# Two-layer graph network over 128 graphs: graph layers beside the next group's first feed-forward, attention two groups ahead beside the second

## The chip, the cores and the metric

The kernel runs on one core of one Trainium2 chip. The metric is the device time of one execution in microseconds (us), lower is better. The engines are called as the profile calls them: PE is TensorE (matmuls), PEld its weight loads, DVE is VectorE, ACT is ScalarE, POOL is GpSimd, SP is SyncE, which here only issues DMAs.

## The reference, cut

The input holds 128 graphs of 128 nodes with 256 features, and one 0/1 adjacency matrix for each graph. Layer 0 is an attention whose values are chosen by the adjacency entry (four relations, of which 0 and 1 occur), followed by a feed-forward with Gelu. Layer 1 is two graph-attention steps in a row, followed by a feed-forward with Relu. Each half of a layer ends in a layer norm. All is float32.

```python
# layer 0; h = 8 heads of dh = 32
scores = jnp.einsum('bhid,bhjd->bhij', q, k) / np.sqrt(dh)
attn = jax.nn.softmax(scores, axis=-1)
for r in range(Wv.shape[0]):
    v_r = (src @ Wv[r] + bv[r]).reshape(Bb, Nn, h, dh).transpose(0, 2, 1, 3)
    mask = (adj_matrix == r)[:, None]
    out = out + jnp.einsum('bhij,bhjd->bhid', attn * mask, v_r)
attn_out = out.transpose(0, 2, 1, 3).reshape(Bb, Nn, Dm) @ Wo + bo
x = _ln(src + attn_out, g1, beta1)
ff = jax.nn.gelu(x @ W1 + b1, approximate=False) @ W2 + b2
return _ln(x + ff, g2, beta2)

# layer 1
def _gat(h, adj, W, a, out_features):
    Wh = jnp.matmul(h, W)
    e = Wh @ a[:out_features] + jnp.swapaxes(Wh @ a[out_features:], 1, 2)
    e = jax.nn.leaky_relu(e, negative_slope=ALPHA)
    att = jax.nn.softmax(jnp.where(adj > 0, e, NEG), axis=1)
    return jnp.matmul(att, Wh)
h = _gat(_gat(x, adj, W1, a1, Fout), adj, W2, a2, W2.shape[1])
h = _layernorm(x + h, g_ln1, b_ln1)
ff = jnp.matmul(jax.nn.relu(jnp.matmul(h, w_ff1) + b_ff1), w_ff2) + b_ff2
return _layernorm(h + ff, g_ln2, b_ln2)
```

## The kernel before

The 128 graphs are taken in 32 groups of four (G = 4), so a group is 512 tokens. A group runs through these stages; "unit" is the kernel's word for a piece of a feed-forward.

- Projections (in `layer0`): two matmul pairs for q, two for k (`pq`, L382, emptied by ACT at L386) and four for the values of relation 0 and of the difference of relations 1 and 0 (`pv`, L392, emptied by DVE at L396).
- Attention (`scores`, `attended`), twice, each for two graphs: scores for four head groups into four tiles `ps` (L319), exponential on ACT (L326), product with the adjacency on DVE (L327), sums with a matrix of ones (`pden`, L342), weighted values (`pav`, L352), reciprocal (L359) and product (L362) on DVE. Then the output projection `pwo` in two halves (L412), each added to the residual on DVE (`added`, L270) into `t0`.
- Layer norm (`normed`): statistics on DVE (L237, L238), the power −0.5 on POOL (L241), subtraction and product on DVE (L243). `scaled` makes the residual of the next stage on POOL (L250, L251), `transposed` turns the normed tile for the next matmuls: eight transposes on PE into two tiles `pt` (L260), each emptied by ACT (L263).
- Feed-forward (`ffn`): eight units `ph` of two matmuls (L280), each followed by Gelu or Relu on ACT (L284), then two halves `po` of four units (L291), each half added by DVE.
- Graph layer (`layer1`): `pw` and `pb` (L452, L459), a chain of edge scores (`edges`: ACT L423, DVE L426, ACT exponential L427, DVE L430 to L436, POOL L437), `py` and `pb` (L467, L471), a second chain of edge scores, and `pg` (L482), added into `t2`.

PE's order is written out by hand (`manual_schedule` for PE alone); a scheduler orders the other engines' queues at build time, and each queue runs in order on the chip. `beside` interleaves: the side generator yields how many units of the feed-forward come next. In the main loop (L541), turn g pairs the first feed-forward of group g with the attention of group g + 1 (`turn`, with the transposes of group g − 1 after the four q and k projections), then the second feed-forward of group g − 1 with the graph layer of group g. So at g = 0 the graph layer has nothing beside it, nor has the first group's attention.

PSUM tiles are of [128, 512] float32. Pool `ps_s` has four (tag `s`: `ps`, `pt`, `pw`, `py`, `pg`), `ps_mm` two (tag `mm`: `pq`, `pv`, `ph`, `po`, `pwo`), and `ps_av` one for tag `av` and one for `den`. A tile's place is taken again when the engine that empties it is done.

At the start the weights are loaded on SP's queue, the bias vectors as rows and columns on ACT's queue; at the end of these loads come the weights of the graph layer (L191, L192), from which DVE and PE make combined weights (L193 to L219) ahead of all other PE work. The residual `res`, `t` and the transposed `yT` tiles have three buffers each, `hT` one.

At the end a check of sums and variances is reduced to one flag (L567 to L590); a general version of the kernel runs only if the flag is set.

Of the kernel before, what the change touches and what calls it, by code (L numbers as in the profile page):

```python
# [10 lines left out]
F32 = mybir.dt.float32  # L11
# [14 lines left out]
G = 4  # L26
# [4 lines left out]
class Weights:  # L31


    def __init__(self, tc, const, a):
        self.tc, self.nc, self.const, self.a = tc, tc.nc, const, a

# [10 lines left out]
    def col(self, name):  # L47
        v = self.a[name]
        t = self.tile([P, v.shape[0] // P], "c_" + name)
        with self.nc.allow_non_contiguous_dma(reason="a bias vector as columns"):  # L50
            self.nc.scalar.dma_start(t, v.rearrange("(c p) -> p c", p=P))
        return t

    def row(self, name, first=None, t=None):
        v = self.a[name]
        n = 1
        for s in v.shape:
            n *= s
        n = first or n
        if t is None:  # L60
            t = self.tile([P, n], "r_" + name)
        self.nc.scalar.dma_start(
            t, bass.AP(tensor=v.tensor, offset=v.offset, ap=[[0, P], [1, n]])
        )
        return t
# [38 lines left out]
def fast_pass(ctx, tc, a, out):  # L104
# [27 lines left out]
    def load(g):  # L132
        xt = io.tile([P, NCH, T], F32, tag="xT", name=f"xT_{g}")
        nc.sync.dma_start(
            xt, xT[:, g * T : (g + 1) * T].rearrange("(c p) t -> p c t", p=P)
        )
        ad = w3p.tile([P, G, P], I32, tag="adj", name=f"adj_{g}")
        nc.sync.dma_start(ad, adjT[:, g * G : (g + 1) * G, :])
        xr = io.tile([P, G, D], F32, tag="x", name=f"x_{g}")
        nc.sync.dma_start(  # L140
            xr, x[g * T : (g + 1) * T, :].rearrange("(b p) d -> p b d", p=P)
        )
        return xt, ad, xr


    k.constants()
    wq, wk = k.w("L0_gnn_Wq"), k.w("L0_gnn_Wk")
    first = dict(zip(("xt", "ad", "xr"), load(0)), g=0)
# [3 lines left out]
    for c in range(NCH):  # L152
        nc.sync.dma_start(
            wv[:, c], a["L0_gnn_Wv"][0:2, c * P : (c + 1) * P, :].rearrange("r p n -> p r n")
        )
        nc.vector.tensor_sub(wv[:, c, 1], wv[:, c, 1], wv[:, c, 0])
    bv = k.row("L0_gnn_bv", 2 * D)
    nc.vector.tensor_sub(bv[:, D:], bv[:, D:], bv[:, :D])
    wo, bo = k.w("L0_gnn_Wo"), k.row("L0_gnn_bo")
    w1, b1 = k.w("L0_gnn_W1"), k.col("L0_gnn_b1")  # L160
    w2 = k.w("L0_gnn_W2")
    g1c, be1c = k.col("L0_gnn_g1"), k.col("L0_gnn_beta1")
    g2c, be2c = k.col("L0_gnn_g2"), k.col("L0_gnn_beta2")
    g1r = k.row("L0_gnn_g1")

    be1b2 = k.row_sum("L0_gnn_beta1", "L0_gnn_b2")
    g2r, be2r = k.row("L0_gnn_g2"), k.row("L0_gnn_beta2")
# [13 lines left out]

    temp = flat(w1p.tile([P, NF, T], F32, tag="hT", name="temp"))
    taken = [0]

    def cut(*shape):
        n = math.prod(shape)
        taken[0] += n
        t = temp[:, taken[0] - n : taken[0]]
        return t.rearrange("p (c n) -> p c n", c=shape[0]) if len(shape) > 1 else t

    gw1, gw2 = (k.w("L1_gnn_W" + s, cut(NCH, D)) for s in "12")  # L191
    a1, a2 = (k.row("L1_gnn_a" + s, t=cut(2 * D)) for s in "12")  # L192
    scr = cut(D)  # L193
    wa1 = k.columns(gw1, a1, scr, "1")
    wa2 = k.columns(gw2, a2, scr, "2")
    rhs = cut(NCH, D + 2)
    nc.vector.tensor_copy(rhs[:, :, :D], gw2)
    nc.vector.tensor_copy(rhs[:, :, D : D + 1], wa2[:, :, 1:2])
    nc.vector.tensor_copy(rhs[:, :, D + 1 : D + 2], wa2[:, :, 0:1])
    gw1T = cut(NCH, D)  # L200
    for m in range(NCH):
        pt = mm_tile(f"pgt_{m}")
        for c in range(NCH):
            nc.tensor.transpose(
                pt[:, c * P : (c + 1) * P], gw1[:, c, m * P : (m + 1) * P], k.ident
            )
        nc.scalar.copy(gw1T[:, m, :], pt[:, :D])
    wu = k.tile([P, NCH, NU], "wu")
    wb = k.tile([P, NCH, P], "wb")
    for m in range(NCH):  # L210
        pu = mm_tile(f"pgw_{m}")
        for c in range(NCH):
            nc.tensor.matmul(
                pu[:, : D + 2], gw1T[:, c, m * P : (m + 1) * P], rhs[:, c, :],
                start=(c == 0), stop=(c == NCH - 1),
            )
        nc.scalar.copy(wu[:, m, : D + 2], pu[:, : D + 2])
        nc.vector.tensor_copy(wu[:, m, D + 2 :], wa1[:, m, 1:2])
        nc.vector.tensor_copy(wb[:, m, :], wa1[:, m, 0:1].to_broadcast([P, P]))  # L219
# [28 lines left out]
    def scaled(y, gr, br, n):  # L248
        o = w3p.tile([P, G, D], F32, tag="res", name="res_" + n)
        nc.gpsimd.tensor_mul(o, y, over(gr))  # L250
        nc.gpsimd.tensor_add(o, o, over(br))  # L251
        return o
# [21 lines left out]
    def ffn(t, inT, wa, ba, func, wb_, res, n):  # L274

        hT = w1p.tile([P, NF, T], F32, tag="hT", name="hT_" + n)
        for f in range(NF):
# [7 lines left out]
            yield  # L285
        for p in range(G // 2):
# [13 lines left out]
    def beside(main, side):  # L300

        for units in side:
            for _ in range(units):
                next(main, None)
        for _ in main:
            pass
# [26 lines left out]
    def attended(S, p):  # L333
# [5 lines left out]
        for u in range(2):  # L339
            for c in range(NCH):  # L340
                for s in range(HC):
                    nc.tensor.matmul(  # L342
                        pden[s * DH : (s + 1) * DH, u, c, :], k.ones, e[:, s, u, c, :],
                        start=True, stop=True,
                    )
# [20 lines left out]
    def layer0(S):  # L366
# [10 lines left out]
        for o, w, bias in (("qT", wq, bq), ("kT", wk, bk)):  # L377
            S[o] = w1p.tile([P, NCH, T], F32, tag=o, name=f"{o}_{n}")
            for m in range(NCH):
# [7 lines left out]
                yield 1  # L387
        for b in range(G):
# [8 lines left out]
            yield 1  # L397
        S["oT"] = oT = w1p.tile([P, NCH, T], F32, tag="oT", name="oT_" + n)
        scores(S, 0)
        yield 2  # L400
        attended(S, 0)
        scores(S, 1)
        yield 2
        attended(S, 1)
        S["t0"] = t = w3p.tile([P, G, D], F32, tag="t", name="t0_" + n)
        for p in range(G // 2):
            yield 2
# [8 lines left out]
            added(t, p, po, xr)  # L416
# [23 lines left out]
    def layer1(S, after):  # L440

        n = str(S["g"])
        normed(S["t1"], "1_" + n)
        res = scaled(S["t1"], g2r, be2r, "1_" + n)
        yield 4
        yT = transposed(S["t1"], g2c, be2c, "1_" + n)
        yield 1
# [13 lines left out]
        after()  # L461
        yield 5
# [13 lines left out]
        yield 5  # L476
        S["t2"] = t = w3p.tile([P, G, D], F32, tag="t", name="t2_" + n)
        for p in range(G // 2):
# [6 lines left out]
            added(t, p, po, res)  # L485

    def norm0(S):
        n = "0_%d" % S["g"]
        normed(S["t0"], n)
        S["res0"] = scaled(S["t0"], g1r, be1b2, n)  # L490

    def norm2(S):
        n = "2_%d" % S["g"]
        normed(S["t2"], n)
        S["res2"] = scaled(S["t2"], h1r, he1c2, n)

    def written(S):

        g = S["g"]
        normed(S["t3"], f"3_{g}", c_out[:, g])  # L500
        o = scaled(S["t3"], h2r, he2r, f"3_{g}")
        nc.sync.dma_start(
            out[g * T : (g + 1) * T, :].rearrange("(b p) d -> p b d", p=P), o
        )

    def first_ffn(S):
        S["t1"] = t = w3p.tile([P, G, D], F32, tag="t", name="t1_%d" % S["g"])
        return ffn(t, S["x1T"], w1, b1, AF.Gelu, w2, S["res0"], "0_%d" % S["g"])

    def second_ffn(S):  # L510
        S["t3"] = t = w3p.tile([P, G, D], F32, tag="t", name="t3_%d" % S["g"])
        return ffn(t, S["x3T"], u1, c1, AF.Relu, u2, S["res2"], "1_%d" % S["g"])
# [4 lines left out]
    def entered(g):  # L517
        return dict(zip(("xt", "ad", "xr"), load(g)), g=g)

    def x1T(S):  # L520
        S["x1T"] = transposed(S["t0"], g1c, be1c, "0_%d" % S["g"])

    def x3T(S):
        S["x3T"] = transposed(S["t2"], h1c, he1c, "2_%d" % S["g"])

    def turn(S, prev):

        side = layer0(S) if S else iter(())
        for i in range(4):
            yield next(side, 1)  # L530
        if prev:
            x3T(prev)
        yield from side

    with tc.manual_schedule(engines={mybir.EngineType.PE}):
        cur, prev = first, None
        for _ in layer0(cur):
            pass
        norm0(cur)
        x1T(cur)  # L540
        for g in range(NG):  # L541
            nxt = entered(g + 1) if g + 1 < NG else None
            if prev:
                norm2(prev)
            beside(first_ffn(cur), turn(nxt, prev))

            def after():
                if nxt:
                    x1T(nxt)

            side = layer1(cur, after)
            if nxt:
                first_units = next(side)
                norm0(nxt)
                side = itertools.chain([first_units], side)
            beside(second_ffn(prev) if prev else iter(()), side)
            if prev:
                written(prev)
            prev, cur = cur, nxt
        norm2(prev)  # L560
        x3T(prev)
        for _ in second_ffn(prev):
            pass
        written(prev)
# [356 lines left out]
```

## Time and profile before

| | us |
|---|---|
| median of 3 runs (3091.01 to 3093.69) | 3093.62 |
| the profiled execution | 3091.51 |
| its span, first to last instruction | 3089.7 |
| mean granted clock of PE | 0.992 of full |
| L280 `ph`, 128x512, one record of two passes | 594 ns, 429 ns from one to the next |
| L291 `po`, 128x256, one record | 379 to 384 ns |
| L326 exponential, 128x512 | 603 ns |
| ACT_TABLE_LOAD, 64 of them | 1283 ns |
| L359 reciprocal, 128x512 | 3349 ns |
| L250, L251 on POOL, 128x1024 | 2353 to 2395 ns |

A matmul of float32 appears as two records, since it makes two passes. Records of PE overlap: what counts is the distance from one start to the next, which the timeline shows. A row of the timeline has the start and the duration in us, engine, line, operation, output<-input, shape, and the number of merged instructions; in brackets stands the engine's idle time before it, if there was any, and what ended it. In the list of waits, a row gives who waited for whom: us in total, how often, the longest. A row of windows gives the stretch, its length, the busy time of PE, PEld, DVE, ACT and POOL, PE's granted clock, the DMA share and GB/s.

### The profile page before, as it was taken

The numbers are of one execution on the slowest core, as the hardware profiler recorded it, in microseconds if no ns is written. First come the engines' busy times: TensorE is split into PE (matmuls) and PEld (weight loads), VectorE is DVE, ScalarE is ACT, GpSimd is POOL, SyncE is SP. The second block draws the span as 40 slices with busy tenths as digits, with TensorE's granted clock in tenths as the row PEclk, the third lists the DMA queues.
The fourth block names the chain that finished last, engine by engine and source line by source line (L and its number), as shares of the span: only waits on it lengthen the run. The fifth ranks groups of instructions, "written<-read, shape, count | busy, mean of one in ns | idle before, by whom it ended". The sixth has DMA issues, their size and how long they took to land.

```text
span 3089.7 us, 42733 instructions
## 1 busy us (share of the span) xinstructions
PE 2998.7 (97%) x18062; PEld 2018.5 (65%) x18062; DVE 1571.7 (51%) x3434; ACT 989.0 (32%) x1733; POOL 881.5 (29%) x488
## 2 busy tenths in 40 slices
PE   3989999999999999999999999999999999999996
PEld 2556676666676666676666676666676666676664
DVE  3444564554554554554554554554555554554523
ACT  1223333323333323333233333233333233333331
POOL 0213322313322313322323322323323223322222
PEclk9999999999999999999999999999999999999998
DMA  4000000000000000000000000000000000000000
GB/s 152 21 12 23 18 18 25 21 18 25 18 18 22 24 18 25 18 18 21 25 18 25 18 18 21 25 18 24 18 18 21 25 18 25 18 18 8 8 7 15
DMA packets 58101, 69.80 MB, mean 23 GB/s; under 512 B 6704, under 2 KB 44720, under 8 KB 57904
## 3 DMA queue, kind: packets, MB, share of 16 engines
q1 hardware_dynamic: 51632, 64.76, 6.9%
q8 instruction: 144, 2.36, 0.3%
q10 hardware_dynamic: 6272, 2.25, 0.3%
q14 instruction: 53, 0.43, 0.0%
HBM read 50.22 MB, written 16.78 MB: 22 GB/s over the span
## 4 chain that ended last, share of the span: by engine, by line
PE 94%; issue 3%; DMA 1%; DVE 1%; POOL 1%; ACT 0%; POOLq 0%; DVEq 0%; ACTq 0%
PE po L291 29%; PE ph L280 28%; PE pq L382 7%; PE pv L392 7%; PE pw L452 4%; PE pav L352 4%; PE pwo L412 3%; PE pt L260 3%; PE ps L319 2%; PE pden L342 2%; PE py L467 2%; PE pg L482 2%; PE pb L459 2%; PE pb L471 1%; DVE t L243 0%
## 5 line engine op out<-in xcount | busy, mean ns | idle before, releaser
L241 POOL TENSOR_TENSOR rs<-rs,mhalf 128x4 f32<-128x4 f32 x128 | 134.0, 1053 | 1610.6 <-DVE rs L240 1610.6
L280 PE MATMUL ph<-yT,w_L_gnn_W 128*128 128x512 f32 x1024 | 481.9, 594 | 0.0
L291 PE MATMUL po<-w_L_gnn_W,hT 128*128 128x256 f32 x2048 | 472.1, 384 | 0.0
L291 PE MATMUL po<-w_L_gnn_w_ff,hT 128*128 128x256 f32 x2048 | 457.5, 379 | 0.0
L280 PE MATMUL ph<-yT,w_L_gnn_w_ff 128*128 128x512 f32 x1024 | 456.5, 594 | 0.0
L291 PEld LDWEIGHTS po<-w_L_gnn_w_ff,hT 128*128 128x128 f32 x2048 | 386.5, 190 | 65.3 <-issue 14.8
L291 PEld LDWEIGHTS po<-w_L_gnn_W,hT 128*128 128x128 f32 x2048 | 381.4, 190 | 62.2 <-issue 6.6
L284 ACT ACTIVATE hT<-ph,c_L_gnn_b_ff 128x512 f32<-128x512 f32 x256 | 175.4, 685 | 684.6 <-PE ph L280 684.6
L243 DVE TENSOR_SCALAR t<-t,mv,rs 128x256 f32<-128x256 f32 x384 | 319.3, 893 | 126.2 <-POOL rs L241 126.2
L280 PEld LDWEIGHTS ph<-yT,w_L_gnn_W 128*128 128x128 f32 x1024 | 195.2, 191 | 245.5 <-issue 230.8
L396 DVE TENSOR_TENSOR v<-pv,r_L_gnn_bv 128x512 f32<-128x512 f32 x128 | 88.5, 691 | 484.4 <-PE pv L392 484.4
L280 PEld LDWEIGHTS ph<-yT,w_L_gnn_w_ff 128*128 128x128 f32 x1024 | 188.2, 191 | 205.4 <-issue 186.6
L284 ACT ACTIVATE hT<-ph,c_L_gnn_b 128x512 f32<-128x512 f32 x256 | 175.9, 687 | 441.3 <-PE ph L280 440.9
L392 PE MATMUL pv<-wv,xT 128*128 128x512 f32 x512 | 240.2, 592 | 0.0
L359 DVE RECIPROCAL rd<-pden 128x512 f32<-128x512 f32 x64 | 214.3, 3349 | 20.8 <-PE pden L342 20.7
L327 DVE TENSOR_TENSOR pm<-e,adj 128x512 f32<-128x512 f32 x256 | 159.5, 685 | 114.3 <-ACT e L326 114.3
L237 DVE BATCH_NORM_STATS2 st<-t 128x6 f32<-128x256 f32 x512 | 192.5, 413 | 5.5
L437 POOL TENSOR_TENSOR gs<-gs,gr 128x512 f32<-128x512 f32 x64 | 66.5, 1039 | 426.3 <-DVE gr L436 415.0
L326 ACT ACTIVATE e<-ps 128x512 f32<-128x512 f32 x256 | 132.1, 603 | 152.0 <-PE ps L319 151.7
L250 POOL TENSOR_TENSOR res<-t,r_L_gnn_g 128x1024 f32<-128x1024 f32 x64 | 150.8, 2357 | 87.2 <-DVE t L243 87.2
L392 PEld LDWEIGHTS pv<-wv,xT 128*128 128x128 f32 x512 | 94.9, 190 | 108.1 <-issue 108.1
L250 POOL TENSOR_TENSOR res<-t,r_L_gnn_g_ln 128x1024 f32<-128x1024 f32 x64 | 153.3, 2395 | 31.4 <-DVE t L243 31.4
(101 smaller groups left out, 3633.5 us busy)
## 6 DMA issues: line engine op xcount, KB each, us to landing
xT<-in_xT_dram SPq DMA_DIRECT2D x32, 512.0 KB, 3.7
x<-in_x_dram SPq DMA_DIRECT2D x32, 512.0 KB, 3.9
out_dram<-res SPq DMA_DIRECT2D x32, 512.0 KB, 2.9
adj<-in_adjT_dram SPq DMA_DIRECT2D x32, 256.0 KB, 2.7
w_L_gnn_W<-in_L_gnn_W_dram SPq DMA_DIRECT2D x2, 1024.0 KB, 9.1
w_L_gnn_w_ff<-in_L_gnn_w_ff_dram SPq DMA_DIRECT2D x2, 1024.0 KB, 9.5
wv<-in_L_gnn_Wv_dram SPq DMA_DIRECT2D x2, 256.0 KB, 7.8
temp<-in_L_gnn_a_dram ACTq DMA_DIRECT2D x2, 256.0 KB, 7.5
```

What stands on the lines that cost most here:

```text
L237: nc.vector.bn_stats(st[:, b, :], t[:, b, :])
L241: nc.gpsimd.tensor_tensor(rs, rs, k.mhalf, op=ALU.pow)
L243: nc.vector.tensor_scalar(t[:, b, :], t[:, b, :], mv[:, b, 0:1], rs[:, b : b + 1], op0=ALU.subtract, op1=ALU.mult,)
L250: nc.gpsimd.tensor_mul(o, y, over(gr))
L280: nc.tensor.matmul(ph, wa[:, c, f * P : (f + 1) * P], inT[:, c, :], start=(c == 0), stop=(c == NCH - 1),)
L284: nc.scalar.activation(hT[:, f, :], ph, func, bias=ba[:, f : f + 1])
L291: nc.tensor.matmul(po[:, s * D : (s + 1) * D], hT[:, f, b * P : (b + 1) * P], wb_[:, f, :], start=(f == 0), stop=(f == NF - 1),)
L326: nc.scalar.activation(e[:, s], pss[s], AF.Exp, scale=SCALE)
L327: nc.vector.tensor_mul(pm[:, s], e[:, s], ad[:, 2 * p : 2 * p + 2, None, :].to_broadcast([P, 2, NCH, P]),)
L359: nc.vector.reciprocal(rd, pden)
L382: nc.tensor.matmul(pq, w[:, c, m * P : (m + 1) * P], xt[:, c, :], start=(c == 0), stop=(c == NCH - 1),)
L392: nc.tensor.matmul(pv, xt[:, c, b * P : (b + 1) * P], wv[:, c].rearrange("p r d -> p (r d)"), start=(c == 0), stop=(c == NCH - 1),)
```

## The change

The order of work is rewritten; what is computed stays.

- Loads: xT of group 0 is first on SP's queue, then Wq, Wk and Wv, then adjacency and x, then the graph layer's weights, then the rest in order of use. After `bo`, rows and columns go over SP's queue too. Making the graph layer's combined weights becomes a generator whose two steps are placed between the parts of the first attention.
- `layer0` is split into `projections` and `attention`; `beside` becomes `in_order`, which takes a list of steps: an integer runs so many units, a function is called, a generator is advanced by one step.
- Main loop: turn g pairs the first feed-forward of group g + 1 with the graph layer of group g (its first two steps), and the second feed-forward of group g with the projections and attention of group g + 2 and the graph layer's last step.
- The sums `pden` are made by four matmuls of 512 columns instead of sixteen of 128.
- The output norm is written in place (`scaled` gets the tile `t3` as its output); for the last group it is done graph by graph, all but the power on DVE, with a DMA each.

```diff
     k.constants()
+    first = {"g": 0}
+    first["xt"] = load_xT(0)
     wq, wk = k.w("L0_gnn_Wq"), k.w("L0_gnn_Wk")
-    first = dict(zip(("xt", "ad", "xr"), load(0)), g=0)
     bq, bk = k.col("L0_gnn_bq"), k.col("L0_gnn_bk")
...
+    bv = k.row("L0_gnn_bv", 2 * D)
+    first["ad"], first["xr"] = load_rest(0)
+    for c in range(NCH):
         nc.vector.tensor_sub(wv[:, c, 1], wv[:, c, 1], wv[:, c, 0])
-    bv = k.row("L0_gnn_bv", 2 * D)
     nc.vector.tensor_sub(bv[:, D:], bv[:, D:], bv[:, :D])
-    wo, bo = k.w("L0_gnn_Wo"), k.row("L0_gnn_bo")
+    bo = k.row("L0_gnn_bo")
+
+    k.queue = nc.sync
...
+    gw1, gw2 = (k.w("L1_gnn_W" + s, cut(NCH, D)) for s in "12")
+    a1, a2 = (k.row("L1_gnn_a" + s, t=cut(2 * D)) for s in "12")
+    wo = k.w("L0_gnn_Wo")
+    g1c, be1c = k.col("L0_gnn_g1"), k.col("L0_gnn_beta1")
     w1, b1 = k.w("L0_gnn_W1"), k.col("L0_gnn_b1")
+    g1r = k.row("L0_gnn_g1")
+
+    be1b2 = k.row_sum("L0_gnn_beta1", "L0_gnn_b2")
...
-    def beside(main, side):
-
-        for units in side:
-            for _ in range(units):
-                next(main, None)
-        for _ in main:
+    def in_order(ffn_, *steps):
+
+
+        for s in steps:
+            if isinstance(s, int):
+                for _ in range(s):
+                    next(ffn_, None)
+            elif callable(s):
+                s()
+            else:
+                next(s, None)
+        for _ in ffn_:
...
-        for u in range(2):
-            for c in range(NCH):
-                for s in range(HC):
-                    nc.tensor.matmul(
-                        pden[s * DH : (s + 1) * DH, u, c, :], k.ones, e[:, s, u, c, :],
-                        start=True, stop=True,
-                    )
+        for s in range(HC):
+            nc.tensor.matmul(
+                pden[s * DH : (s + 1) * DH], k.ones, e[:, s], start=True, stop=True
+            )
...
+    def attention(S):
+
+        n = str(S["g"])
         S["oT"] = oT = w1p.tile([P, NCH, T], F32, tag="oT", name="oT_" + n)
         scores(S, 0)
-        yield 2
+        yield
         attended(S, 0)
         scores(S, 1)
-        yield 2
+        yield
         attended(S, 1)
-        S["t0"] = t = w3p.tile([P, G, D], F32, tag="t", name="t0_" + n)
+        yield
+        S["t0"] = t = w3p.tile([P, G, D], F32, tag="t", name="t_0_" + n)
...
+            added(t, p, po, S["xr"])
+            yield
...
+    def norm(S, i, part=None):
+
+        n = f"{i}_{S['g']}"
+        if part in (None, 0):
+            normed(S[f"t{i}"], n)
+        if part in (None, 1):
+            S[f"res{i}"] = scaled(S[f"t{i}"], *rows[i], n)
+
+    def turned(S, i):
+        S[f"x{i + 1}T"] = transposed(S[f"t{i}"], *cols[i], f"{i}_{S['g']}")
...
+    def written_by_graph(S):
+
+        g, t = S["g"], S["t3"]
+        for b in range(G):
+            n = f"3_{g}_{b}"
+            st = small.tile([P, 6], F32, tag="st", name="st_" + n)
+            mv = c_out[:, g, b, :]
+            nc.vector.bn_stats(st, t[:, b, :])
+            nc.vector.bn_aggr(mv, st)
+            rs = small.tile([P, 1], F32, tag="rs", name="rs_" + n)
+            nc.vector.tensor_scalar(rs, mv[:, 1:2], EPS, None, op0=ALU.add)
+            nc.gpsimd.tensor_tensor(rs, rs, k.mhalf[:, :1], op=ALU.pow)
+            nc.vector.tensor_scalar(
+                t[:, b, :], t[:, b, :], mv[:, 0:1], rs, op0=ALU.subtract, op1=ALU.mult
+            )
+            nc.vector.tensor_mul(t[:, b, :], t[:, b, :], h2r)
+            nc.vector.tensor_add(t[:, b, :], t[:, b, :], he2r)
+            r0 = g * T + b * P
+            nc.sync.dma_start(out[r0 : r0 + P, :], t[:, b, :])
...
-        cur, prev = first, None
-        for _ in layer0(cur):
-            pass
-        norm0(cur)
-        x1T(cur)
-        for g in range(NG):
-            nxt = entered(g + 1) if g + 1 < NG else None
-            if prev:
-                norm2(prev)
-            beside(first_ffn(cur), turn(nxt, prev))
-
-            def after():
-                if nxt:
-                    x1T(nxt)
-
-            side = layer1(cur, after)
-            if nxt:
-                first_units = next(side)
-                norm0(nxt)
-                side = itertools.chain([first_units], side)
-            beside(second_ffn(prev) if prev else iter(()), side)
-            if prev:
-                written(prev)
-            prev, cur = cur, nxt
-        norm2(prev)
-        x3T(prev)
-        for _ in second_ffn(prev):
-            pass
-        written(prev)
+        st = [first, entered(1)] + [None] * (NG - 2)
+        none, steps = iter(()), graph_weights()
+        at = attention(first)
+        in_order(none, *[projections(first)] * 8, at, steps, at, steps, at, at, at)
+        norm(first, 0)
+        turned(first, 0)
+        pr, at = projections(st[1]), attention(st[1])
+        in_order(
+            first_ffn(first), *[pr, 1] * 8, at, 2, at, 2, at, 2, at, at, lambda: norm(st[1], 0), 2
+        )
+        norm(first, 1)
+        turned(st[1], 0)
+        for g in range(NG - 1):
+            S, S1 = st[g], st[g + 1]
+            graph = layer1(S)
+            if g + 2 < NG:
+                st[g + 2] = S2 = entered(g + 2)
+                if g == 0:
+                    head = (4, lambda: turned(S, 1), 2)
+                else:
+                    head = (6,)
+                in_order(
+                    first_ffn(S1),
+                    *(() if g == 0 else (lambda: written(st[g - 1]),)),
+                    *head, graph, 6, graph, 4,
+                )
+                pr, at = projections(S2), attention(S2)
+                norm(S1, 1, 0)
+                in_order(
+                    second_ffn(S), pr, pr, graph, lambda: norm(S, 2), lambda: norm(S1, 1, 1),
+                    *[pr] * 6, lambda: turned(S1, 1), lambda: turned(S, 2),
+                    at, 3, at, 3, at, 3, at, at, lambda: norm(S2, 0), 6, lambda: turned(S2, 0),
+                )
+            else:
+                in_order(
+                    first_ffn(S1), lambda: written(st[g - 1]),
+                    graph, 5, graph, 5, graph, lambda: norm(S, 2), 5, lambda: turned(S, 2),
+                )
+                graph = layer1(S1)
+                norm(S1, 1)
+                in_order(
+                    second_ffn(S), 4, lambda: turned(S1, 1), 1, graph, 5, graph, 5, graph,
+                    lambda: norm(S1, 2),
+                )
+                written(S)
+                turned(S1, 2)
+                in_order(second_ffn(S1))
+                written_by_graph(S1)
```

## The prediction

> **What bounds the kernel now.** I read the page first, then TensorE's waits, then its timeline, which tells whether TensorE waits anywhere between start and end.
>
> ```profile
> span 3089.7 us, 42733 instructions
> PE 2998.7 (97%) x18062; PEld 2018.5 (65%) x18062; DVE 1571.7 (51%) x3434; ACT 989.0 (32%) x1733; POOL 881.5 (29%) x488
> PE   3989999999999999999999999999999999999996
> ```
> ```profile
> PE pgt L204 <- DMA temp<-in_L_gnn_W_dram: 37.8, 1, 37.8
> PE pt L260 <- DVE t L243: 17.1, 7, 5.1
> PE py L467 <- POOL gs L437: 6.6, 1, 6.6
> PE pg L482 <- POOL gs L437: 5.2, 1, 5.2
> ```
>
> TensorE is busy in all slices but the first and last; its waits are single events. The timeline, at the first projection of four turns (some lines between left out):
>
> ```profile
> 48.31 3.66 PE L382 MATMUL pq<-xT,w_L_gnn_Wq 128*128 128x512 f32 x8
> ...
> 86.32 3.41 PE L382 MATMUL pq<-xT,w_L_gnn_Wq 128*128 128x512 f32 x4
> ...
> 174.20 2.15 PE L382 MATMUL pq<-xT,w_L_gnn_Wq 128*128 128x512 f32 x4
> ...
> 1568.62 1.88 PE L382 MATMUL pq<-xT,w_L_gnn_Wq 128*128 128x512 f32 x4
> ```
> ```profile
> 1661.57 1.88 PE L382 MATMUL pq<-xT,w_L_gnn_Wq 128*128 128x512 f32 x4
> ```
> ```profile
> 2869.86 1.88 PE L382 MATMUL pq<-xT,w_L_gnn_Wq 128*128 128x512 f32 x4
> ```
>
> A middle turn takes 1661.57 − 1568.62 = 92.95 us, and TensorE's timeline has no idle entry in it. So the ledger of the span is: 48.3 before the first projection, 38.0 for the first attention alone, 87.9 for the second turn, 29 × 92.95 = 2695.7, and 219.8 from 2869.86 to the end. Of the 3089.7, 32 × 92.95 = 2974.4 is dense work; 115.3 is start, end and single waits. A new order can win only there, and it can lose in every turn.
>
> **What the Trainium skill says.** "PSUM — Partial Sum Buffer", Specifications: eight banks of 2 KiB per partition. Each tile here (512 f32) is one bank: four for tag `s`, two for `mm`, one each for `av` and `den`; none is spare. "SBUF — State Buffer", section "SBUF: two separate sides": VectorE and GpSimd share a port pair under an exclusive lock. The trace agrees: four L243 took 1.38 us with GpSimd idle, 5.50 beside L250/L251. "TensorE: Matmul & The Clock Gate", Part 1: TensorE drops to half clock when it idles for much of a 3.4 us window. Here the 1.81 us gap before 143.02 was enough: the granted clock in 140 to 150 us is 0.83, so 0.17 × 10 = 1.7 us are lost.
>
> ```profile
> 140.00:150.00 10.00, 8.17 (x31) 5.84 (x30) 5.94 (x17) 2.68 (x5) 6.94 (x5) 0.83 0.18 52
> ```
>
> **Part 1: start, first turns and end (gain).**
> Loads. L204 stood ahead of all on TensorE and waited 37.85 us for the graph weights. Afterwards xT and Wq come first: in before's trace Wq landed at 4.65 us, xT (third in line) at 8.6; I take the first projection at 8, bounds 6 and 13, against 48.3. Wv, adj, x and the graph weights follow; L204 is needed only after scores 0, at about 8 + 8×1.72 + a cold clock 1.7 + 1.1 = 25, by when about 5 MB have landed at the 200 to 270 GB/s of before's first slices. SP now issues the columns and rows too: some 20 issues of 0.4 us, past which xT_1 must get; all loads with xT_1 are some 10.5 MB, and before moved more than that by 43 us; xT_1 is wanted at 49. So nothing, or up to 3 us if SP is slow.
> The first attention took 38.0; plus the cold start 1.7 and about 1 for the graph-weight matmuls that don't fit in its gaps (0.67 and 2.49): 41, ending at 49, not 86.3.
> Second turn: 86.32 to the last output projection's end (139.31 + 1.73) is 54.7; a bank wait (below) adds 1.05. Transposes of norm 0 then wait for add, statistics, power and L243: in before 1528.22 to 1532.62 for the add and what follows, 4.66 with the 0.26 from TensorE to VectorE; two units of 1.72 cover 3.4, so 1.3, then 0.87. At 107.
> Graph layer 0 ran alone in before (waits 6.57, 5.25 and 0.55). It now lies beside the first feed-forward of group 1: 27.5 (16 units × 1.716) + 3.51 + 1.72 + 2.63 of graph matmuls + 0.87 = 36.2. At 143. The rest of a turn is 92.95 − 35.3 = 57.6: at 201. Then 29 turns, 2695.6: at 2896.
> End: two passes of feed-forward with graph layer and transposes, 2 × 37.9; 0.5 for the denser edge chains; last transposes wait 4 (chain 4.66 less one unit of 1.72, plus GpSimd's power for group 30, 1.05); 0.9; cold 1.7; last feed-forward 27.5; tail 9. The tail was 3089.7 − 3075.1 = 14.6, with 2.34 + 2.34 on GpSimd over whole groups; row blocks on VectorE (about 0.4 each) save about 5. Sum 119: **3015** without new waits in the turns, 75 less than now (65 to 85).
>
> **Part 2: 512-column sums.** pden went 32 records in batches of four, 0.109 apart: 8 × 0.109 = 0.87 us. Four 512-wide matmuls have two passes; a pass of 512 columns takes 0.429 (L280): 0.86. I take nothing; at best the 0.14 between pden and pav goes (64 × 0.14 = −9); at worst the four column groups don't run together at this width (8 × 0.429, +164).
>
> **Part 3: the 30 full turns (loss).** Nothing is added to the work, so each turn costs 92.95 plus what TensorE waits.
>
> (a) *Transposes ahead of scores.* Two `turned` now stand directly before `scores`. They take all four `s` banks; scores 0 wants all four in its first four matmuls. TensorE spends 2 × 0.87 = 1.74 on them; the banks come free by four L263 on ACT.
>
> ```profile
> 1536.61 1.04 PE L260 MATMUL pt<-ident,t 128*128 128x128 f32 x8
> ...
> 1544.42 1.04 PE L260 MATMUL pt<-ident,t 128*128 128x128 f32 x8
> ```
> ```profile
> 1537.39 1.44 ACT L263 ACTIVATE yT<-pt,c_L_gnn_beta,c_L_gnn_g 128x512 f32<-128x512 f32 x2
> ```
>
> Two take 1.44 and one 0.787, so they start 0.65 apart. The first starts 0.44 + 0.26 = 0.70 in, the fourth ends at 0.70 + 3×0.65 + 0.79 = 3.44; with the weight load (0.19) scores start at about 3.6 instead of 1.8: **1.8** (1.5 to 2.0). Behind scores stand all of TensorE's work, and the exponentials for them. In before, eight units lay between.
>
> (b) *Two output projections in a row.* Three units after attended 1 are f6, f7 and the first quarter of `po`, which keeps one of two `mm` banks. pwo 0 takes the other; pwo 1 must wait until VectorE has emptied it:
>
> ```profile
> 1524.83 0.69 DVE L270 TENSOR_TENSOR t<-pwo,x 128x512 f32<-128x512 f32 x1 [0.66 <-PE pwo L412]
> ```
>
> pwo 0's stream ended at 1522.84 + 1.73, so 0.26 + 0.69 + about 0.1: **1.05** (0.9 to 1.3). Before had two units between them.
>
> (c) *Values in a row.* Eight projections without feed-forward units give VectorE 1.72, not 3.44, to empty a bank. From the end of the first feed-forward: t1 is normed at 4.7, so `scaled` holds GpSimd until 9.4; t2 is added by 6.1, its statistics and rs are through at 9.5 (rs shares the port), power to 10.6, four L243 to 12.0. v 0 ends at 10.3 on TensorE, v 2 wants its bank at 12.05. If v 0's add is queued behind the L243s it ends at 12.7: 0.8; ahead of them, 0. I take **0.6**; up to 1.6 if GpSimd blocks the L243s.
>
> (d) *Exp between Gelus.* Beside the graph layer the feed-forward is now Gelu, not Relu. Edge chain 1's exp stands among f6 and f7, so two more table loads (1.283 each in this trace) a turn. If Gelu f6 is queued first, Gelu f7 ends 6.6 us after pb, and po wants it at 3.44 + 7 × 0.43 = 6.45: 0.2. If exp is first, f6's bank comes free at 5.3 instead of 3.44: 2.0. I take **0.3**. The edge chains themselves have 10.3 us of cover and need about 8.
>
> (e) *Clock.* The 1.8 of (a) is over half a 3.4 us window if it falls in one; the phase drifts, so in about 4 of 10 turns 1.7 is lost: **0.7** (0 to 1.7).
>
> Per turn 1.8 + 1.05 + 0.6 + 0.3 + 0.7 = 4.45; × 30 = 133. Span 3015 + 133 = 3148. The profiled execution took 3091.51 with a span of 3089.7, so 1.8 more, and the median of the runs is 2.1 above it: **3152**. The turn from loss to gain is at 75/30 = 2.5 us a turn.
>
> **Rivals.**
> 1. *Forecast*, 3.3 to 5.8 a turn: 3118 to 3193. Chance 0.50.
> 2. *The two bank waits alone*: values, table and clock cost nothing; 2.5 to 3.3: 3094 to 3118, with 2.85 giving 3015 + 85 + 4 = 3104. For it: (c) and (d) hang on queue orders that I can't see. 0.15.
> 3. *Faster: the start decides.* The first projection comes 40 us earlier and the graph layer's lone waits go; if ACT and VectorE hand banks back in under 2.5 us a turn, this outweighs them. With 1 us a turn: 3015 + 30 + 4 = 3049 (3019 to 3085). For it: the 37.85 wait is certain to go, engines other than TensorE are half idle. Against it: the four-bank count. 0.22.
> 4. *Queues against it*: exp first (2.0), L243s blocked (1.6), clock each turn; 1.8 + 1.05 + 1.6 + 2.0 + 1.5 = 8 at most: 3194 to 3259. 0.10.
> 5. *512 columns not concurrent*: 3280 and more. 0.03.
>
> **Numbers.** Within 0.2% (3087.4 to 3099.8) is about what a measurement of this kernel can't tell from no change. Rival 3 is faster (0.22, and 0.01 of others), 0.05 falls within, from rival 2; slower 0.72. Forecast's own range: 3118 to 3193. For 8 in 10: below 3055 lies half of rival 3 (0.11), above 3205 most of 4 and 5 (0.09).
>
> **What would show it.** First projection at 8 us; turns of 97 instead of 92.95; ps waiting for ACT's L263 rows and pwo for VectorE's add once a turn; pv waiting for v; four table loads a turn; a granted clock below 0.99. A turn that stays at 93 would make the forecast wrong, and shows rival 3.

## The result and the profile after

The changed kernel takes 3107.32 us (median of 4 runs, 3106.48 to 3108.67) against 3092.59 for the kernel before on the same chip (4 runs, 3091.01 to 3093.69): a ratio of 1.0048, with a 95% interval of 1.0031 to 1.0066. It is slower, as forecast, but by 14.7 us and not by 60. The profiled run took 3106.48 with a span of 3104.7. That lies in the range of the second rival, "The two bank waits alone" (3094 to 3118, with 3104 as its example).

The first lines of the page after:

```profile
span 3104.7 us, 39594 instructions
PE 3038.4 (98%) x16526; PEld 1996.7 (64%) x16526; DVE 1349.4 (43%) x3445; ACT 1077.0 (35%) x1797; POOL 866.9 (28%) x489
PE   8999999999999999999999999999999999999998
```

TensorE is busier than before (98% against 97%) over a longer span. A busy share can't show this loss: waiting is spread over all turns, and part of it is counted as busy, as will be seen. TensorE's waits after (total us, how often, the longest):

```profile
PE pwo L436 <- DVE t L285: 24.3, 31, 0.8
PE ps L342 <- ACT yT L278: 11.1, 60, 0.2
PE pt L275 <- DVE t L257: 7.7, 2, 4.6
PE pq L402 <- DMA w_L_gnn_Wq<-in_L_gnn_Wq_dram: 6.1, 1, 6.1
```

The 37.8 us for the graph weights are gone; in their place stand 6.1 for Wq. New are two waits that come once or twice in every turn: pwo for VectorE's add, and ps for ACT's evacuation of the transposes. There is no row for pv. The first projections of groups 0 and 1, from TensorE's timeline after (start, duration, engine, line, operation, and in brackets the idle time before it with what ended it):

```profile
6.10 6.70 PE L402 MATMUL pq<-xT,w_L_gnn_Wq 128*128 128x512 f32 x8 [6.10 <-DMA w_L_gnn_Wq<-in_L_gnn_Wq_dram]
47.88 2.81 PE L402 MATMUL pq<-xT,w_L_gnn_Wq 128*128 128x512 f32 x4
```

The first attention starts at 6.1 instead of 48.3. Against that, a full turn (from one first `pw` to the next) takes 95.67 us, where it took 92.94: 2.73 more, 30 times, 82 in all. The start and end have gained 3089.7 − (3104.7 − 82) = 67.

The turn's two losses, from the same timeline in the middle of the run:

```profile
1593.75 1.91 PE L275 MATMUL pt<-ident,t 128*128 128x128 f32 x16
1595.59 0.78 PE L342 MATMUL ps<-qT,kT 32*128 32x128 f32 x4
1596.55 0.48 PE L342 MATMUL ps<-qT,kT 32*128 32x128 f32 x2 [0.18 <-ACT yT L278]
1597.22 1.15 PE L342 MATMUL ps<-qT,kT 32*128 32x128 f32 x26 [0.18 <-ACT yT L278]
1598.30 5.42 PE L296 MATMUL ph<-yT,w_L_gnn_w_ff 128*128 128x512 f32 x12
...
1620.85 1.89 PE L436 MATMUL pwo<-w_L_gnn_Wo,oT 128*128 128x256 f32 x8
1623.52 1.99 PE L436 MATMUL pwo<-w_L_gnn_Wo,oT 128*128 128x256 f32 x8 [0.78 <-DVE t L285]
```

Sixteen transposes and 32 scores occupy TensorE from 1593.75 to 1598.30, 4.55 us. Undisturbed they take 1.74 and 1.10 (the scores as in e3), so 1.71 is lost, while the two idle entries add up to 0.36. The rest hides in the groups' modelled durations: four scores take 0.96 until the next group starts, and the next two 0.67, which is the pace at which ACT empties banks. Two output projections take 2.67 from start to start instead of 1.73, and the second one's stream is stretched by 0.1: about 1.05, with 0.78 of it shown as idle. So a wait row tells which wait it is; its price is read from start to start.

### The profile page after: what moved, and what is told of

Its sections match the earlier page's. It is cut to its first block, busy times and chain, and to the rows that moved or that the text cites. A ratio compares the mean times of both kernels' runs of the same rounds, so it can differ in the third digit from the quotient of the medians.

```text
span 3104.7 us, 39594 instructions
## 1 busy us (share of the span) xinstructions
PE 3038.4 (98%) x16526; PEld 1996.7 (64%) x16526; DVE 1349.4 (43%) x3445; ACT 1077.0 (35%) x1797; POOL 866.9 (28%) x489
## 4 chain that ended last, share of the span: by engine, by line
PE 94%; ACT 3%; DVE 1%; DMA 1%; POOL 0%; SPq 0%; issue 0%; ACTq 0%; DVEq 0%; POOLq 0%
PE po L308 29%; PE ph L296 28%; PE pq L402 7%; PE pv L412 7%; PE pwo L436 4%; PE pw L473 4%; PE pav L372 3%; ACT yT L278 3%; PE ps L342 2%; PE pden L363 2%; PE py L487 2%; PE pb L480 2%; PE pg L502 2%; PE pt L275 2%; PE pb L491 1%; DVE t L285 1%
## 5 line engine op out<-in xcount | busy, mean ns | idle before, releaser
L296 PE MATMUL ph<-yT,w_L_gnn_w_ff 128*128 128x512 f32 x1024 | 466.1, 603 | 0.0
L308 PE MATMUL po<-w_L_gnn_W,hT 128*128 128x256 f32 x2048 | 460.9, 381 | 1.3 <-ACT hT L300 1.3
L296 PE MATMUL ph<-yT,w_L_gnn_W 128*128 128x512 f32 x1024 | 451.6, 592 | 2.4 <-ACT hT L300 2.0
L278 ACT ACTIVATE yT<-pt,c_L_gnn_beta,c_L_gnn_g 128x512 f32<-128x512 f32 x128 | 92.6, 773 | 721.6 <-PE pt L275 721.5
L285 DVE TENSOR_TENSOR t<-po,res 128x512 f32<-128x512 f32 x128 | 88.5, 691 | 445.7 <-PE po L308 445.7
L412 PE MATMUL pv<-wv,xT 128*128 128x512 f32 x512 | 225.4, 592 | 0.0
L451 DVE SCALAR_TENSOR_TENSOR gs<-gs 128x512 f32<-128x512 f32 x64 | 44.6, 697 | 412.9 <-ACT gs L448 412.8
L257 DVE TENSOR_SCALAR t<-t,mv,rs 128x256 f32<-128x256 f32 x384 | 132.6, 409 | 112.5 <-POOL rs L255 112.5
```

The lines of the kernel that those rows point to most:

```text
L257: nc.vector.tensor_scalar(t[:, b, :], t[:, b, :], mv[:, b, 0:1], rs[:, b : b + 1], op0=ALU.subtract, op1=ALU.mult,)
L278: nc.scalar.activation(yT[:, c, :], pt, AF.Identity, bias=bc[:, c : c + 1], scale=gc[:, c : c + 1])
L296: nc.tensor.matmul(ph, wa[:, c, f * P : (f + 1) * P], inT[:, c, :], start=(c == 0), stop=(c == NCH - 1),)
L308: nc.tensor.matmul(po[:, s * D : (s + 1) * D], hT[:, f, b * P : (b + 1) * P], wb_[:, f, :], start=(f == 0), stop=(f == NF - 1),)
L412: nc.tensor.matmul(pv, xt[:, c, b * P : (b + 1) * P], wv[:, c].rearrange("p r d -> p (r d)"), start=(c == 0), stop=(c == NCH - 1),)
```

## The experiments

None of the variants changes what is computed. The ratios are to the kernel before, run on the same chip alongside. Turn lengths are of the middle turns, from one first `pw` to the next. "After" is the changed kernel, and (a) to (e) are the five losses of the prediction.

### e1: transposes kept away from the scores

```diff
-                    *[pr] * 6, lambda: turned(S1, 1), lambda: turned(S, 2),
+                    pr, pr, lambda: turned(S1, 1), pr, pr, pr, lambda: turned(S, 2), pr,
```

> The two transposes are moved apart, the first behind the two k projections, the second ahead of the last v projection, so one unit of 1.72 us lies between the last transposes and scores. Theory (bank waits): the 1.71 us that scores 0 waits for its s banks go in each of the 30 full turns, the turn falls from 95.67 to about 93.96, the time from 3107 to about 3056. Rival (the turn is held by something behind it, exponentials and products for attended 0): the wait moves to pden or pav and less than half is gained, 3085 or more.

Measured: 3058.95 us, ratio 0.9889 (0.9872 to 0.9905), turn 94.07. One turn is 1.61 shorter than after, and the wait of ps for ACT is gone. (a) is worth 1.6 when it is taken away, and 1.7 as read from the trace of after.

### e2: two units put back between the output projections

```diff
-                    at, 3, at, 3, at, 3, at, at, lambda: norm(S2, 0), 6, lambda: turned(S2, 0),
+                    at, 3, at, 3, at, 3, at, 2, at, lambda: norm(S2, 0), 4, lambda: turned(S2, 0),
```

> Two feed-forward units are put between the two output projections (and four, not six, follow). Theory (bank waits): the 1.05 us that the second output projection waits for VectorE's add go in each turn, turn 94.6, time about 3107 - 31 = 3076. Rival (the norm of t0 is late instead, its cover has shrunk from six units to four, 6.9 us against a chain of 4.7): the transposes of t0 wait and nothing is gained, 3100 or more.

Measured: 3075.17, ratio 0.9944 (0.9927 to 0.9960), turn 94.62, 1.05 shorter. The wait of pwo for the add is gone from the turns. (b) is as computed.

### e3: both

> Both edits together. Theory: the gains add, 30 x 2.76 = 83 us, turn about 92.9 as in the kernel before, time about 3025, some 2% faster than both kernels. Rival (one of the waits only hid another): less than the sum of the two single runs' gains, 3040 or more.

Measured: 3031.47, ratio 0.9800 (0.9784 to 0.9817), turn 93.01. The two gains were 48.4 and 32.2; together they give 75.9, nearly their sum. In the turn they add up: 1.61 and 1.05 alone, 2.66 together. What is missing lies at the two ends, where the profiled execution of e3 has some 10 us more at half clock than that of after. TensorE's four longest waits in e3:

```profile
PE pt L275 <- DVE t L257: 10.0, 2, 7.0
PE pq L402 <- DMA w_L_gnn_Wq<-in_L_gnn_Wq_dram: 6.1, 1, 6.1
PE pflag L636 <- DVE good L634: 5.6, 1, 5.6
PE ph L296 <- ACT hT L300: 2.0, 1, 2.0
```

All are single events again, as in the kernel before, and the turn is back at its old length within 0.07. So the two bank waits are all but 0.07 of what a turn lost on balance (e6 finds a further 0.24, which small gains elsewhere in the turn had covered), and the remaining 61 us below the kernel before are what start and end have gained.

### e5: the residual products of norm 1 directly behind the norm

This builds the queue order that (c) had assumed.

```diff
-                norm(S1, 1, 0)
+                norm(S1, 1)
...
-                    second_ffn(S), pr, pr, graph, lambda: norm(S, 2), lambda: norm(S1, 1, 1),
+                    second_ffn(S), pr, pr, graph, lambda: norm(S, 2),
```

> The norm of t1 is emitted whole, so that GpSimd makes the residual of t1 (two times 2.35 us) before the power for t2, the order that my prediction's step on the values assumed. That step: power and the four L257 for t2 come late, v 0's add stands behind them, and pv waits 0.8 us a turn: 3107 + 24 = 3131. Rival (VectorE has slack even so): no wait of pv, 3107.

Measured: 3132.08 (3128.35 to 3134.66), ratio 1.0122 (1.0107 to 1.0138), turn 96.43, 0.76 longer than after. A wait of pv appears in every turn:

```profile
PE pv L412 <- DVE v L416: 15.4, 31, 0.8
```

GpSimd's timeline in the changed kernel, and then in e5:

```profile
1586.17 1.01 POOL L255 TENSOR_TENSOR rs<-rs,mhalf 128x4 f32<-128x4 f32 x1 [4.69 <-DVE rs L254]
1588.67 2.36 POOL L265 TENSOR_TENSOR res<-t,r_L_gnn_g_ln 128x1024 f32<-128x1024 f32 x1 [1.50 <-DVE t L257]
1590.98 2.36 POOL L265 TENSOR_TENSOR res<-t,r_L_gnn_g 128x1024 f32<-128x1024 f32 x1
```

```profile
1600.36 2.35 POOL L266 TENSOR_TENSOR res<-res,r_L_gnn_beta 128x1024 f32<-128x1024 f32 x1
1602.82 1.02 POOL L255 TENSOR_TENSOR rs<-rs,mhalf 128x4 f32<-128x4 f32 x1
```

In the changed kernel GpSimd had idled for 4.69 us when the variance of norm 2 arrived; it does the power at once, and the products of both norms follow. In e5 it comes to the same power from the products of norm 1 without a pause. VectorE's timeline in the changed kernel and in e5 shows what that does to v:

```profile
1587.21 1.38 DVE L257 TENSOR_SCALAR t<-t,mv,rs 128x256 f32<-128x256 f32 x4 [1.12 <-POOL rs L255]
1588.80 0.69 DVE L416 TENSOR_TENSOR v<-pv,r_L_gnn_bv 128x512 f32<-128x512 f32 x1 [0.20 <-PE pv L412]
```

```profile
1600.86 1.88 DVE L254 TENSOR_SCALAR rs<-mv 128x4 f32<-128x4 f32 x1
1603.87 1.38 DVE L257 TENSOR_SCALAR t<-t,mv,rs 128x256 f32<-128x256 f32 x4 [1.13 <-POOL rs L255]
1605.17 1.28 DVE L416 TENSOR_TENSOR v<-pv,r_L_gnn_bv 128x512 f32<-128x512 f32 x2
```

After, the add of v 0 waits for TensorE. In e5 it waits behind the four L257, and these wait for the power. The small L254 took 1.88 us in e5 and 0.17 after: it started at 1600.86 and ended at 1602.74, when the GpSimd product that began at 1600.36 had ended. This agrees with what the Trainium skill, "SBUF — State Buffer", section "SBUF: two separate sides", says of the port pair that the two engines share: an exclusive lock, held for the whole instruction. The mechanism and the price of (c), 0.8 if the add is queued behind the L257s, are right; its premise on GpSimd's order was not that of the changed kernel.

### e4: the scores' last bank first

An attempt to make the wait of (a) one gap instead of several, to see whether the clock then drops. The edit is in `scores`.

```diff
-                for s in range(HC):
+                for s in reversed(range(HC)):
```

> Scores run the head groups in reverse, so that the first matmul waits for the bank that comes free last; the wait for the s banks keeps its length but is one piece. My prediction's step on the clock: a piece of about 1.7 us lies wholly in a 3.4 us stretch in some 4 to 5 of 10 turns and costs 1.7 us of half clock there, so about 0.7 us a turn, 3107 + 21 = 3128, and the granted clock falls to about 0.985. Rival (what saved the clock was not the crumbs but that 1.7 us are too short): no change, 3107, clock 0.997.

Measured: 3108.03, ratio 1.0050 (1.0034 to 1.0067), turn 95.68, with the same two small gaps of 0.19 and 0.18. The wait stayed in pieces, so this says nothing on the clock.

### e9: one wait of 1.8 us in one piece

Built on e6 (below): the transposes of norm 0 come one unit after the norm, too early by design.

```diff
-                    at, 3, at, 3, at, 3, at, 2, at, lambda: norm(S2, 0), 4, lambda: turned(S2, 0),
+                    at, 3, at, 3, at, 3, at, 2, at, lambda: norm(S2, 0), 1, lambda: turned(S2, 0), 3,
```

> On top of the seven units ahead, the transposes of t0 come one unit behind the second output projection instead of four, so TensorE idles for VectorE's norm in each turn: about 1.9 us in one piece and 0.7 more between the transposes (chain to the first L257 3.6 us after the projection's end, one unit of 1.72 of cover). Question: does such an idle take the clock down, when the 1.7 us in pieces ahead of scores did not in any turn? If idle time over half of a 3.4 us stretch is what counts, 4 to 7 of 10 turns lose 1.7 us more: turns of 95.4 and 97.1 mixed, about 3023 + 30 x 2.6 + 30 = 3130, a dozen and more entries of half clock in the turns. If even this is too little, all turns are alike at 95.4 and the time is about 3100.

Measured: 3106.03, ratio 1.0044 (1.0028 to 1.0061). Most turns take 95.44, 2.67 more than in e6: 1.81 in one piece and about 0.86 between the transposes. Three of the 30 take 96.8, 1.36 more; in these, and in no others, the clock fell to half for 3.41 us.

Which three they are depends on where the gap falls. The trace records when the granted clock changes, and in each of the twelve traces all these changes lie whole multiples of 3.413 us apart, that is, on a grid. In e9 the gap begins 1.16, 1.25 and 1.27 us behind a grid line in the three turns with the drop, and 1.30 to 2.47 behind one in the 27 others. Two neighbours in this order, at 1.27 and at 1.30: for each, the grid step that holds the gap and the next one (columns: stretch and length, then busy time with the number of instructions of PE, PEld, DVE, ACT and POOL, granted clock, DMA share, GB/s), and then both on TensorE's timeline:

```profile
765.68:769.09 3.41, 1.60 (x8) 0.91 (x6) 2.81 (x10) 0.00 (x0) 1.02 (x1) 1.00 0.43 143
769.09:772.50 3.41, 3.41 (x11) 2.82 (x12) 1.46 (x6) 2.17 (x3) 2.75 (x2) 0.50 0.03 11
1721.40:1724.81 3.41, 1.59 (x8) 0.94 (x6) 2.81 (x10) 0.00 (x0) 1.02 (x1) 1.00 0.40 140
1724.81:1728.22 3.41, 3.41 (x18) 2.78 (x18) 1.50 (x6) 2.35 (x3) 2.71 (x2) 1.00 0.04 14
```

```profile
768.76 2.29 PE L275 MATMUL pt<-ident,t 128*128 128x128 f32 x8 [1.81 <-DVE t L257]
...
1724.52 1.73 PE L275 MATMUL pt<-ident,t 128*128 128x128 f32 x8 [1.81 <-DVE t L257]
```

The step with the gap holds 1.60 us of work in one turn and 1.59 in the other, but only the first is followed by half clock (11 matmul records against 18 in the next step), and its eight transposes took 2.29 instead of 1.73. A turn of 95.44 is 27.96 grid steps, so the gap begins 0.13 earlier on the grid in each turn. Once it begins at 1.27 or before, the drop makes the turn 1.36 longer, which puts the next gap at 2.4 or later, and it takes some ten turns to come down again. So with even more idle time than (e) supposed, the drop comes in 1 turn of 10, which is 0.14 us a turn, not 0.7.

### e6: the graph layer's step one unit later, upon e3

```diff
-                    head = (4, lambda: turned(S, 1), 2)
+                    head = (4, lambda: turned(S, 1), 3)
...
-                    head = (6,)
+                    head = (7,)
...
-                    *head, graph, 6, graph, 4,
+                    *head, graph, 5, graph, 4,
```

> On top of both bank edits, seven Gelu units stand ahead of the graph layer and five behind it, so that only one Gelu lies between the two exponentials. Theory: the 0.24 us that po waits behind the table loads in each turn go, and two table loads a turn with them: 3031 - 7 = 3024, ACT_TABLE_LOADs from 128 to about 68. Rival (the edge chain loses its cover, five units, 8.6 us, against a chain of about 7): py waits for GpSimd, no gain or a loss.

Measured: 3022.9, ratio 0.9774 (0.9759 to 0.9789), turn 92.77, 0.24 shorter than in e3. ACT's table loads, by line, in the changed kernel and in e6 (busy us and mean ns | idle before):

```profile
L300 ACT ACT_TABLE_LOAD x64 | 82.1, 1283 | 1.2
L452 ACT ACT_TABLE_LOAD x63 | 80.8, 1283 | 1.1
```

```profile
L300 ACT ACT_TABLE_LOAD x34 | 43.6, 1283 | 0.6
L452 ACT ACT_TABLE_LOAD x33 | 42.3, 1283 | 0.6
```

Two loads a turn are gone with one unit moved, and with them 0.24 us a turn: the two loads of 2.57 us on ACT had cost TensorE only that much. ACT's timeline in the changed kernel says why:

```profile
1655.76 0.69 ACT L300 ACTIVATE hT<-ph,c_L_gnn_b 128x512 f32<-128x512 f32 x1 [0.50 <-PE ph L296]
1656.46 1.28 ACT L452 ACT_TABLE_LOAD   x1
1657.75 0.63 ACT L452 ACTIVATE gs<-gs 128x512 f32<-128x512 f32 x1
1658.40 1.28 ACT L300 ACT_TABLE_LOAD   x1
1659.70 0.69 ACT L300 ACTIVATE hT<-ph,c_L_gnn_b 128x512 f32<-128x512 f32 x1
```

Gelu f6 comes first, so its bank is free in time; only Gelu f7 is late. That is the cheap one of the two cases in (d).

### e7: the kernel before, with 512-column sums only

```diff
-        for u in range(2):
-            for c in range(NCH):
-                for s in range(HC):
-                    nc.tensor.matmul(
-                        pden[s * DH : (s + 1) * DH, u, c, :], k.ones, e[:, s, u, c, :],
-                        start=True, stop=True,
-                    )
+        for s in range(HC):
+            nc.tensor.matmul(
+                pden[s * DH : (s + 1) * DH], k.ones, e[:, s], start=True, stop=True
+            )
```

> The kernel before with the 512-column sums alone. Theory (column groups run together at 512 too): 8 x 0.109 = 0.87 becomes 2 x 0.429 = 0.86, and the second attention's pden and pav may go from 2.90 to 2.75: 3092 - 0 to 5. Rival (wider matmuls don't overlap): plus 164.

Measured: 3093.61 (13 runs) against 3092.98, ratio 1.0001 (0.9993 to 1.0009). A row of its timeline (line 340) beside one of the kernel before (line 342):

```profile
1511.34 1.07 PE L340 MATMUL pden<-e,ones 128*32 128x512 f32 x8
```

```profile
1508.87 1.08 PE L342 MATMUL pden<-e,ones 128*32 128x128 f32 x32
```

A quarter of the instructions takes the same time. Neither the gain of 9 nor the loss of 164 is there. The second `pden` with its `pav`, for which a fall from 2.90 to 2.75 was possible, takes 2.97 here, and a turn 93.03 instead of 92.94.

### e8: the kernel before, with the new order of loads only

The edit is the change's own loading part (xT and Wq first, rows and columns on SP's queue, `graph_weights` stepped between the parts of the first attention) in front of the old main loop. The end of it, cut:

```diff
-        for _ in layer0(cur):
-            pass
+        steps = graph_weights()
+        for i, _ in enumerate(layer0(cur)):
+            if i in (8, 9):
+                next(steps, None)
```

> The kernel before with the changed load order and the graph layer's weights made between the parts of the first attention, the main loop as before. Theory: the first projection comes at 6 instead of 48 us and the second turn's at 48 instead of 86: 3092 - 38 = 3054. Rival (later turns give it back, because weights or the next group arrive late): 3065 or more.

Measured: 3055.7, ratio 0.9881 (0.9866 to 0.9896), turn 92.94 as before. The first projection stands at 6.09 instead of 48.31, 42.2 earlier, of which 37.3 reach the end. This part alone beats the kernel before; of the 67 that start and end gained in the whole change, it accounts for more than half. The other 30 (the graph layer of group 0 no longer alone, and the end) no run takes apart.

### e10: projections ahead of the first transposes, upon e6

```diff
-        turned(first, 0)
...
-            first_ffn(first), *[pr, 1] * 8, at, 2, at, 2, at, 2, at, at, lambda: norm(st[1], 0), 2
+            first_ffn(first), pr, pr, pr, lambda: turned(first, 0), *[1, pr] * 5, 3, at, 2, at, 2,
+            at, 2, at, at, lambda: norm(st[1], 0), 2,
```

> On top of the seven units ahead, three of group 1's projections come before the first transposes of group 0, in the wait of 4.6 to 7 us for the first norm. Theory (work that needs no norm fills the wait, and xT_1, landed at 40 in the changed kernel, is there): 5 us less, about 3018. Rival (xT_1 lands late or the norm is slower beside the loads): no gain, 3023.

Measured: 3014.53, ratio 0.9751 (0.9735 to 0.9767): the fastest of all, 77.6 us under the kernel before and 92.8 under the changed one. The two waits of pt for L257, 8.8 in e6, are down to one of 3.1. The gain on e6 is 8.4, where 5 was expected: with the wait at the start gone, the 6.83 us of half clock that followed it in e6 are gone too, and these had cost some 3.4, half of their length.

## Why the prediction was right in its sign and wrong in its size

The forecast of the span was 3015 + 30 × 4.45 = 3148.5; the trace has 3104.7. The 43.8 between them, term by term:

| term of the sum | predicted | measured | effect on the span |
|---|---|---|---|
| base without new waits | 3015 | 3104.7 − 30 × 2.73 = 3022.8 | +7.8 |
| (a) transposes ahead of scores | 1.8 | 1.71 | −2.7 |
| (b) two output projections in a row | 1.05 | 1.05 | 0 |
| (c) values in a row | 0.6 | 0 | −18 |
| (d) exp between Gelus | 0.3 | 0.24 | −1.8 |
| (e) clock | 0.7 | 0 | −21 |
| other joints of a turn | 0 | 2.73 − 3.00 = −0.27 | −8.1 |

**The steps that failed are (c) and (e): 39 of the 43.8.**

(c) said: "t1 is normed at 4.7, so `scaled` holds GpSimd until 9.4", and from there counted the power for t2, the L243s and v 0's add. But in the changed list of steps `norm(S1, 1, 0)` stands ahead of the projections and `norm(S1, 1, 1)`, which holds `scaled`, behind `norm(S, 2)`. In the trace GpSimd has nothing to do for 4.69 us and then does the power at once, so the last L257 ends at 1588.6 and v 0's add starts at 1588.80 with its operand. e5 restores the assumed order and shows 0.76 a turn, beside the 0.8 that was computed for it. The arithmetic was right, and the split that made it void was in the text of the change.

(e) took it that the gap of (a), "over half a 3.4 us window if it falls in one", would cost 1.7 in about 4 turns of 10. That half a window is enough was inferred from one event of the kernel before, and e9 shows that it is not: ten of its 30 gaps of 1.81 us lie wholly within one grid step, and seven of these leave the clock at full. What decided there was where in the step the gap began. The Trainium skill, "TensorE: Matmul & The Clock Gate", Part 1, gives a window of 3413 ns that runs free of the kernel, and the grid of the traces agrees with that; it names an idle window as what brings the clock down, but in e9 the drop came behind steps with 1.60 us of work, so there the measurement decides.

In the changed kernel's trace no turn has an entry of half clock; there are three in all, at 46, 3060 and 3098 us. Its turn of 95.67 is 28.03 grid steps, and the transposes of (a) begin at 30 places from 0.05 to 3.36 behind a grid line, so it was not a lucky place that spared it. Whether it is that the wait comes in pieces, or that it is shorter than in e9 (1.71 against 1.81 and 0.86), stays open: e4 was meant to tell and could not.

**What held.** (a) and (b) were computed from the count of banks and the spacing of the evacuations; e1 and e2 take each away alone, and e3 shows that they are independent. (d) took a value near the cheap case, and this is the case that the ACT queue has; the prediction could not see that order, so that it came close is partly luck. 512-column sums at nothing: e7. The start: first projection at 6.1 (taken: 8), second turn at 47.88 (taken: 49).

**Base.** It came out 7.8 higher, and nearly all of that lies behind the last full turn. The first projection of group 2 stands at 143.16, where the sum had 143 (the single steps before it were off by 1 to 2 us both ways). From 2977.77 to the end the trace has 126.9, where 119 was put: in the last turn TensorE waits 1.96 and 1.29 for Gelu, where 0.5 was put; the tail from 3092.9 takes 11.8, where 9 was put; the last transposes wait 3.1, where 4 was put, and they and the feed-forward behind them, with 6.83 us at half clock, take 31.7, where 30.1 was put.

**Other joints.** The three losses found in a turn add up to 3.00 and the turn grew by 2.73. With the 1.61 of e1 for (a) they are 2.90, and e6, which has none of the three, shows the rest alone: its turn is 92.77, 0.17 under the kernel before. Some 0.15 of it is the second pden with its pav, 2.75 instead of 2.90 us. The 512 columns alone did not bring that (2.97 in e7); its cause is not shown.

The break-even of 2.5 us a turn was nearly met: 2.73 against (3089.7 − 3022.8) / 30 = 2.23. Of the forecast's five losses two followed from counts and the other three depended on queue orders or on where a gap falls. Adding a middle value for each of these pushed the sum past what came: the two, and the cheap form of (d).

Not tried: filling the two waits for Gelu in the last turn, filling the last transposes' wait of 3.1 that e10 keeps, and a shorter tail.

## What to carry to other kernels

When stages are put side by side, count the banks each wants at the seam and the pace at which they are emptied: that count gave both real losses to within 0.1 us, and a few steps moved at the seams turned a kernel 0.5% slower into one 2.0% faster. Before a delay on another engine's queue is priced, read in the program which step stands ahead on that queue. Losses that hang on such an order are better kept as bounds than added at middle values. A gap that comes back every turn meets the clock's grid at another place each time: ask how far it moves per turn before a share of the turns is priced.

## What was not expected of the hardware

Whether a gap of about 2 us in TensorE's work halves the clock depends on where it begins on a grid of 3.413 us. The twelve traces have 45 gaps of 1.81 to 2.09 us that begin at full clock. The ten that begin 0.42 to 1.27 us behind a grid line are all followed by half clock; the 35 that begin 1.30 to 3.23 behind one are not. The wait of 1.96 us for Gelu in the last turn, which nine traces have, is among them: with a drop in e3 and e5 (0.78 and 1.10), without one in the other seven (1.66 to 3.23). So is the kernel before's wait of 2.09 us near its end: with a drop there (0.42), without one in e7 (2.99). A drop cost 1.36 us in e9 and 1.69 in e3. The eleven gaps of 2.49 and 3.10 us were all followed by one, wherever they began (0.20 to 3.27). A gap's beginning is the modelled end of a matmul, so the border near 1.3 can be shifted by a constant; what amount of work in a grid step decides is not shown.

A wait for a bank shows in the wait rows with much less than it costs: 0.36 of 1.71 for ps, 0.78 of 1.05 for pwo, 0.49 of 0.76 for pv in e5. The rest is in lengthened groups of matmuls that count as busy.

After a table load the next activation starts 1.29 us after the load's start (1656.46 to 1657.75), so nothing beyond the load's own 1.28 us was lost.
